# A decoder layer on one core: 64-column products in a row in the first and last units of cross-attention, and a softmax's exponential and two experts' weight casts in another place on ScalarE

## The chip, the cores and the metric

The kernel runs on one core of a Trainium2 chip. Its time is the device time of one execution in microseconds (us). A core has a matrix engine (TensorE, PE in the profile), a vector engine (VectorE, DVE), an engine for activations and copies (ScalarE, ACT), a general one (GpSimd, POOL) and one that issues most of the transfers here (SyncE, SP). Each engine takes its instructions strictly in order. An instruction that waits holds up all that is behind it on its engine. So in a kernel of this kind, where all engines work at once on different stages, the order of the instructions on each engine is a large part of the design. The change that is studied here is one of order alone.

## The reference

One decoder layer on x with 1024 tokens of width 256, in float32 (cut to what matters here):

```python
x = x + self_attention(layernorm(x))      # 16 heads of 128, weights as mxfp4 codes and scales
# cross-attention, latent form; context c: 64 rows per sequence, 64 wide
q_hk  = layernorm(x) @ Wq.T               # 16 heads of 128
q_big = einsum('bshk,hkq->bshq', q_hk, w_kc_q)        # 192 wide a head
q_big = q_big * cos_q + rotate_half(q_big) * sin_q    # rotary embedding
q_r   = q_big @ W_qr ;  kv = (c rotated)  @ W_kr      # 64 wide
p     = softmax(q_r . kv)
x     = x + (p @ c ...) @ Wo.T
# mixture of experts: 16 experts, in 4 groups; top 2 groups, then top 4 experts
xt     = layernorm(x)
scores = softmax(xt @ Wg.T)
g      = max of scores in each group;  experts outside the best 2 groups are masked
topi   = top_k(masked, 4);  w = scores at topi
y      = sum over chosen e of w_e * (silu(xt @ W1[e].T) * (xt @ W3[e].T)) @ W2[e].T
z      = (silu(xt @ Ws1.T) * (xt @ Ws3.T)) @ Ws2.T    # shared expert, inner width 352
out    = x + y + z
```

The inner width of an expert is 176.

## The kernel before, in words

Float32 products are made from pairs: each operand is split into a high part[...] and a low part, the difference. Three products (high by high, high by low, low by high) stand for one. `parts_of` (L111 to L113) makes the split: ScalarE copies the high part, and VectorE subtracts it for the low part. Every product of this kind has line L104 in the profile, and what it computes is told by the names of its tiles.

The stages follow each other: self-attention to about 200 us, cross-attention to about 408, the shared expert and the routing to about 437, then the experts. A scheduler orders each engine's instructions by a planner's estimate of when they are due, and the code corrects it by hand: under `tc.issue_after(m)`, or the shorthand `after(*ms)`, the instructions of a block are ordered behind instruction m. Such an order adds no wait on the chip between engines; it fixes who stands ahead of whom.

*Cross-attention* is cut into eight units: four heads (a "quad") by half of the tokens. The unit loop (L1155 to L1290) has ten turns, n = 0 to 9, and is pipelined: turn n computes the rotated queries of unit n, the scores of unit n - 1 and the context and output projection of unit n - 2. The parts are:

- `rotated_queries` (L990): products with w_q on PE, rotation products rt on VectorE (L1006), their sum `roped` on GpSimd (L1014);
- `pair_queries` (L1025): products with the 64-column matrix w_s (L1032), copied as q_r by ScalarE (L1045);
- `pair_scores` (L1050): scores with 64-column products (L1057), then `softmax` (L325 to L343): maximum sm_m on VectorE, eight exponentials on ScalarE (L331), sums, and the normalised pn on VectorE or GpSimd;
- `transposed` (L352 to L361): transposes of pn on PE, copies by ScalarE;
- `pair_context` (L1065): 64-column products (L1070) to c_t;
- `cross_project` (L1087): products with w_o, added to x on VectorE (L1095).

`layernorm_t` normalises the tokens and transposes them on PE (L216), with the high copy at L222 and the low at L224. In turn n = 0 the second half of the tokens is normalised and transposed for cross-attention. In turns 0 to 6 the 64-column products are ordered by hand in a row. Turns 7, 8 and 9 have a branch of their own with less order. In the late turns routing and the shared expert are woven in: `choose` (L778) picks the experts for a half of the tokens on VectorE: logits lg, group maxima, the top entries, the mask sel (L762); then PE counts earlier choices (L819 from sel, L820 from before), and VectorE works out the target rows `to` (L856). `send` (L860) scatters the tokens to the experts' rows xd in memory by transfers of GpSimd (L864), sixteen of them for the second half. `weights_of_choices` (L891) makes the routing softmax of a half: its maximum r_m (L897), the difference r_p (L899), the exponential on ScalarE (L900), and the chosen weights. silu (L937, L1342) and exp are of different table sets on ScalarE, so a change of function brings an ACT_TABLE_LOAD.

*The experts* (loop from L1407): for each, `expert_weights` loads 640 KB (w, L277), ScalarE casts the high part (L278, 1280 columns), VectorE (experts 0 to 2) or GpSimd subtracts the low (L283). `expert_inputs` (L1308) loads an expert's rows xr from xd (L1314), which waits for the scatters, and transposes them on PE (L1324) into xs; `expert_hidden` (L1333) makes the up products, silu (g, L1342 and L1345) and the product h (L1343, L1346), split as hp; `send_outputs` (L1350) makes the output y and scatters it by GpSimd. Loads of w and xr are issued by SyncE in one order.

Of the kernel before, what the change touches and what calls it, by code (L numbers as in the profile page):

```python
# [30 lines left out]
ALU = mybir.AluOpType  # L31
# [40 lines left out]
def decoder_layer(ctx: ExitStack, tc: tile.TileContext, a: dict, out: bass.AP):  # L72
# [36 lines left out]
        return [(left[0], right[0]), (left[0], right[1]), (left[1], right[0])]  # L109

    def parts_of(src, hi, lo, eng=None):  # L111
        nc.scalar.copy(hi, src)
        return (eng or nc.vector).tensor_tensor(lo, src, hi, ALU.subtract).ins  # L113


    x_pairs = [acts.tile([128, 2, D], F32, tag=f"x{n}", name=f"x{n}") for n in range(NI // 2)]
# [39 lines left out]
    variances, rstds, shifts, highs, lows = [], [], [], [], []  # L156
    norms, scaled, turned, silus, exps, softened = [], [], [], [], [], []

    def layernorm_t(which, halves=(0, 1), rows=None, meanwhile=None):


        xn_t = []
# [1 line left out]
        for half in halves:  # L164
# [47 lines left out]
            for c in range(2):  # L212
                ps = mm_tile() if which == 1 else av_tile()
                for k in range(4):
                    turned.append(
                        nc.tensor.transpose(  # L216
                            ps[:, k * 128 : (k + 1) * 128],
                            xn[k][:, c * 128 : (c + 1) * 128],
                            ident,
                        ).ins  # L220
                    )
                highs.append(nc.scalar.copy(parts[0][:, c, :], ps).ins)  # L222
                lows.append(
                    nc.vector.tensor_tensor(  # L224
                        parts[1][:, c, :], ps, parts[0][:, c, :], ALU.subtract
                    ).ins
                )
            xn_t.append(parts)
# [86 lines left out]
    with ExitStack() as attn:  # L315
# [572 lines left out]
            nc.vector.tensor_tensor(w, w, p, ALU.mult)  # L888
            return w

        def weights_of_choices(half):  # L891


            shape = [128, 4, E]
            lg = logits[half]
            m = fs.tile([128, 4], F32, tag="r_m", name="r_m")
            nc.vector.tensor_reduce(m, lg, AX.X, ALU.max)  # L897
            p = fs.tile(shape, F32, tag=f"r_p{half}", name=f"r_p{half}")
            nc.vector.tensor_tensor(p, lg, m.unsqueeze(2).broadcast_to(shape), ALU.subtract)  # L899
            exps.append(nc.scalar.activation(p, p, AF.Exp).ins)  # L900
            s = fs.tile([128, 4], F32, tag="r_s", name="r_s")
# [79 lines left out]
        with (  # L981
# [179 lines left out]
            for n in range(len(units) + 2):  # L1161
# [4 lines left out]
                roped[n] = []  # L1166
                qd, half = units[min(n, len(units) - 1)]
                rotate = iter(rotated_queries(weights[qd][0], half, roped[n]) if n in here else ())
                with after(*([projected] if n < len(units) - 1 and projected else [])):
                    pts_n = [transposed(pn) for pn in pns.pop(n - 2, ())]  # L1170
                if n < len(units) - 1:
                    roped_done = list(roped_last)
                    order = [m for m in [next(rotate, None)] if m]
                    if n - 1 in here:
# [10 lines left out]
                        c_ts.append(c_t)  # L1185
                    if n == 0:
                        with tc.issue_after(highs[-1]), tc.issue_after(lows[-1]):
                            xn_t += layernorm_t(2, (1,))
                    else:
                        pns[n - 1] = []  # L1190
                        for q_r in q_rs:
                            with after(*order):
                                pn, product = pair_scores(q_r, units[n - 1][1], nc.gpsimd)
                            order = [product]
                            pns[n - 1].append(pn)
                    if n in late:
                        with after(*order):
                            next(prep)
# [4 lines left out]
                else:  # L1203
                    if n - 1 in here:
                        q_rs, _ = pair_queries(weights[units[n - 1][0]][1], roped.pop(n - 1))
                    c_ts = [pair_context(pt, units[n - 2][1])[0] for pt in pts_n]
                    next(rotate, None)
                    if n - 1 in here:

                        eng = nc.gpsimd if n < len(units) else nc.vector  # L1210
                        pns[n - 1] = [pair_scores(q_rs[0], units[n - 1][1], eng)[0]]
                    next(rotate, None)
                    if n - 1 in here:
                        pns[n - 1].append(pair_scores(q_rs[1], units[n - 1][1], eng)[0])
# [32 lines left out]
                if n == 8:  # L1247
                    w_last = dense_weights()
                    with after(exps[-1]):
                        routed.append(weights_of_choices(0))  # L1250
                if n == 9:
                    rows[1] = [
                        xw.tile([128, 3, 2, 2, DC], F32, tag="w_s", name="rows1")
# [326 lines left out]
```

## Time and profile before

| what | us |
|---|---|
| median of 3 runs (lowest and highest) | 556.84 (555.78 to 557.23) |
| the profiled execution | 558.26 |
| its span in the trace | 556.1 |
| PE busy / its share | 524.9 / 94% |
| DVE busy / its share | 382.5 / 69% |
| ACT busy / its share | 304.3 / 55% |
| POOL busy / its share | 228.7 / 41% |
| mean granted PE clock | 0.986 of full speed |

A row of the timeline gives start and length in us, engine, line, operation, output tile, input tiles and shapes, and in brackets the idle time ahead of it with what ended that. Rows of PE's timeline count two records for one product of this kind, so that "x8" is four instructions of the code. A row of stretches gives a piece of the trace and for each engine how long it was busy there, then the clock that was granted to PE, the busy share of the transfer engines and the rate of transfers. "PEld" is the loading of weights into the matrix engine, which overlaps products.

### The profile page before, as it was taken

The numbers are of one execution on the slowest core, as the hardware profiler recorded it, in microseconds if no ns is written. First come the engines' busy times: TensorE is split into PE (matmuls) and PEld (weight loads), VectorE is DVE, ScalarE is ACT, GpSimd is POOL, SyncE is SP. The second block draws the span as 40 slices with busy tenths as digits, with TensorE's granted clock in tenths as the row PEclk, the third lists the DMA queues.
The fourth block names the chain that finished last, engine by engine and source line by source line (L and its number), as shares of the span: only waits on it lengthen the run. The fifth ranks groups of instructions, "written<-read, shape, count | busy, mean of one in ns | idle before, by whom it ended". The sixth has DMA issues, their size and how long they took to land.

```text
span 556.1 us, 10815 instructions
## 1 busy us (share of the span) xinstructions
PE 524.9 (94%) x4013; PEld 442.1 (80%) x4013; DVE 382.5 (69%) x863; ACT 304.3 (55%) x764; POOL 228.7 (41%) x213
## 2 busy tenths in 40 slices
PE   7999999999999989999999999999999879999982
PEld 6888898998989876668677686685886769999971
DVE  5465573754736799657475566758768688999967
ACT  3667575585665520625545364455735377777651
POOL 4260500101000016444342533543534737888873
PEclk9999999999999999999999999999999989999995
DMA  8553432834200779472010000000511577777366
GB/s 227 158 170 109 140 95 77 209 97 133 77 1 1 230 203 306 124 230 73 1 62 12 8 1 1 0 30 2 174 52 71 195 235 265 238 235 262 123 250 217
DMA packets 44263, 70.84 MB, mean 127 GB/s; under 512 B 11824, under 2 KB 25232, under 8 KB 44208
## 3 DMA queue, kind: packets, MB, share of 16 engines
q1 hardware_dynamic: 39376, 58.71, 35.3%
q0 software_dynamic: 3696, 10.36, 4.8%
q10 hardware_dynamic: 1136, 1.05, 0.6%
q8 instruction: 33, 0.54, 0.4%
q14 instruction: 22, 0.18, 0.1%
HBM read 48.61 MB, written 21.86 MB: 127 GB/s over the span
## 4 chain that ended last, share of the span: by engine, by line


## 5 line engine op out<-in xcount | busy, mean ns | idle before, releaser
L1014 POOL TENSOR_TENSOR roped<-rt,rt 128x512 f32<-128x512 f32 x48 | 61.8, 1309 | 52.6 <-DVE rt L1006 51.6
L104 PE MATMUL mm<-xn,w_q 128*128 128x512 f32 x288 | 72.6, 402 | 0.5 <-ACT xn L222 0.5
L1006 DVE TENSOR_TENSOR rt<-mm,rope_q 128x512 f32<-128x512 f32 x96 | 61.0, 680 | 10.8 <-PE mm L104 10.4
L104 PEld LDWEIGHTS mm<-xn,w_q 128*128 128x128 f32 x288 | 52.6, 188 | 14.3 <-issue 1.2
L104 PE MATMUL mm<-xs,w 128*128 128x384 f32 x270 | 53.8, 347 | 6.9 <-issue 2.3
L1363 POOL DMA_INDIRECT yd<-y,to x45 | 47.8, 1062 | 20.7 <-ACT y L1358 7.1
L325 DVE TENSOR_REDUCE sm_m<-at 128x8 f32<-128x512 f32 x32 | 21.9, 684 | 47.9 <-PE at L582 47.1
L104 PEld LDWEIGHTS mm<-xs,w 128*128 128x128 f32 x270 | 46.7, 192 | 9.0 <-issue 5.1
L331 ACT ACTIVATE p<-at,sm_m 128x64 f32<-128x64 f32 x128 | 38.2, 343 | 14.9 <-DVE sm_m L329 12.8
L523 POOL TENSOR_TENSOR wv<-code,scale 128x512 fp32r<-128x512 f32 x7 | 9.1, 1294 | 89.2 <-DMA scale<-in_scales 59.6
L1032 PE MATMUL mm<-roped,w_s 128*64 128x512 f32 x192 | 44.3, 599 | 0.2 <-DVE rt L1006 0.2
L360 ACT COPY pt<-at 64x512 f32<-64x512 f32 x32 | 18.6, 582 | 40.0 <-PE at L352 40.0
L565 ACT ACTIVATE qT<-mm,bqkv 128x512 f32<-128x512 f32 x32 | 21.8, 688 | 33.7 <-PE mm L104 33.7
L104 PE MATMUL mm<-wv,xn 128*128 128x256 f32 x256 | 36.2, 288 | 0.0
L104 PE MATMUL mm<-wo,o 128*128 128x256 f32 x256 | 34.1, 286 | 2.1 <-DVE x L624 2.1
L104 PE MATMUL av<-w,hp 128*128 128x256 f32 x225 | 35.1, 290 | 0.3 <-ACT y L1358 0.3
L104 PEld LDWEIGHTS mm<-wo,o 128*128 128x128 f32 x256 | 31.7, 191 | 3.7 <-DVE x L624 3.2
L104 PE MATMUL mm<-xn,wk 128*128 128x512 f32 x128 | 34.2, 399 | 0.0
L104 PE MATMUL mm<-xn,wq 128*128 128x512 f32 x128 | 33.2, 398 | 0.2
L343 POOL TENSOR_TENSOR pn<-p,sm_s 128x512 f32<-128x512 f32 x14 | 14.6, 1044 | 45.3 <-DVE sm_s L339 45.3
L104 PEld LDWEIGHTS mm<-wv,xn 128*128 128x128 f32 x256 | 32.5, 189 | 0.7
L601 PE MATMUL av<-pt,v 128*128 128x128 f32 x256 | 31.2, 275 | 1.0 <-DVE o L611 1.0
(219 smaller groups left out, 1184.3 us busy)
## 6 DMA issues: line engine op xcount, KB each, us to landing
w<-in_W SPq DMA_DIRECT2D x15, 640.0 KB
code<-in_codes SPq DMA_DIRECT2D x32, 256.0 KB
scale<-in_scales SPq DMA_DIRECT2D x32, 256.0 KB
xr<-xd SPq DMA_DIRECT2D x15, 408.0 KB
xd<-zeros SPq DMA_DIRECT2D x8, 720.0 KB
yd<-zeros SPq DMA_DIRECT2D x8, 512.0 KB
got<-yd SPq DMA_DIRECT2D x16, 256.0 KB
wq<-in_Wq SPq DMA_DIRECT2D x4, 512.0 KB
```

Source lines behind the costliest of these rows:

```text
L104: m = nc.tensor.matmul(ps, lhsT=l, rhs=r, start=(n == 0), stop=(n == len(pairs) - 1))
L325: nc.vector.tensor_reduce(m, sc, AX.X, ALU.max)
L331: last = nc.scalar.activation(p[:, b], sc[:, b], AF.Exp, bias=m[:, b : b + 1], accum_out=s[:, b : b + 1])
L343: .tensor_tensor(pn, p, s.unsqueeze(2).broadcast_to(shape), ALU.mult)
L360: nc.scalar.copy(pt[:S, :, 0, :], ps[:S])
L523: mults[n] = eng.tensor_tensor(w, *loaded[gr].pop(n), ALU.mult).ins
L565: nc.scalar.activation(qk[which][:, half * 512 : (half + 1) * 512], ps, AF.Identity, bias=bqkv[:, which, h : h + 1],).ins
L601: nc.tensor.matmul(av[:, k * 128 : (k + 1) * 128], lhsT=v[:, i, k0 : k0 + HD], rhs=pt[:, i].rearrange("p a q -> p (a q)"), start=True, sto ...
L1006: factors = nc.vector.tensor_tensor(mt, ps3, rope_table(t, 2 * ab + k), ALU.mult)
L1014: nc.gpsimd.tensor_tensor(r.rearrange("p (b s) -> p b s", s=S), one, two, op)
L1032: nc.tensor.matmul(ps[h // 2][(h % 2) * 64 : (h % 2) * 64 + 64], lhsT=w_s[:, t, blk, ab, :], rhs=roped[2 * t + ab], start=first[h], stop=l ...
L1363: sent = nc.gpsimd.indirect_dma_start(out=yd[: (E - 1) * SLOTS + min(TOPK, E - 1 - e) * NT], out_offset=bass.IndirectOffsetOnAxis(ap=to[:, ...
```

## The change

Four things are put in another order. The numbers of instructions on each engine are the same in both kernels.

1. Turn 7 of the unit loop now takes the ordered branch, like turns 0 to 6: its transposes come behind the projection, its queries' products in one row, then contexts and scores in a row. Only turns 8 and 9 remain in the other branch.
2. In turn 0 `layernorm_t` is called with `later=True`: it normalises, but its eight transposes with their copies are returned as a function, which turn 1 calls behind its scores.
3. `parts_of` notes its last high and low instruction. `weights_of_choices` is cut in two: `exps_of_choices` makes the maximum, the difference and the exponential, and for the second half of the tokens it is called in turn 9, ordered behind the casts of the dense expert's hidden; the rest stays in the expert loop.
4. The cast of the weights of expert 1 is ordered behind the last cast of expert 0's input, and that of expert 2 behind the last cast of expert 0's hidden, in both cases instead of behind the last silu. On SyncE the load of expert 3's weights comes to stand ahead of the load of expert 3's inputs.

On PE the order of turn 1 was 2 transposes, a piece of 4 products of L1032, 4 transposes, 4 products, 2 transposes, 4 products, then 16 scores; it is now 12 products, 16 scores, 8 transposes. On ScalarE the exponential of L900 with its table load comes directly behind the last cast of the shared hidden, and the table load back stands directly ahead of the first expert's silu. On VectorE the low part of w_last_up stands ahead of the routing's chain from lg to sel, and the maximum of unit 8's scores behind that chain.

```diff
     def parts_of(src, hi, lo, eng=None):
-        nc.scalar.copy(hi, src)
-        return (eng or nc.vector).tensor_tensor(lo, src, hi, ALU.subtract).ins
+        high_last[0] = nc.scalar.copy(hi, src).ins
+        low_last[0] = (eng or nc.vector).tensor_tensor(lo, src, hi, ALU.subtract).ins
+        return low_last[0]
...
-    def layernorm_t(which, halves=(0, 1), rows=None, meanwhile=None):
+    def layernorm_t(which, halves=(0, 1), rows=None, meanwhile=None, later=False):
...
+            if later:
+                return lambda xn=xn, parts=parts: [turn(xn, parts)]
+            xn_t.append(turn(xn, parts))
...
-        def weights_of_choices(half):
-
+        def exps_of_choices(half):
...
             exps.append(nc.scalar.activation(p, p, AF.Exp).ins)
+            return p
+
+        def weights_of_choices(half, p):
...
-                with after(*([projected] if n < len(units) - 1 and projected else [])):
+                with after(*([projected] if n < len(units) and projected else [])):
                     pts_n = [transposed(pn) for pn in pns.pop(n - 2, ())]
-                if n < len(units) - 1:
+                if n < len(units):
...
-                            xn_t += layernorm_t(2, (1,))
+                            turn_rest = layernorm_t(2, (1,), later=True)
...
+                    if n == 1:
+                        with after(*order):
+                            xn_t += turn_rest()
...
+                        order = [high_last[0]]
                         h_p = dense_gated(*dense_ups)
+
+                        with after(*order, high_last[0], low_last[0], silus[-1]):
+                            p_last = exps_of_choices(1)
...
-            low = lows[-1]
+            low, cast = lows[-1], high_last[0]
             hs[e - 1] = expert_hidden(ws[e - 1], xs[e - 1][0], SLOTS)
+            if e == 2:
+                cast = hidden_high
+            hidden_high = high_last[0]
...
-                with tc.issue_after(low), tc.issue_after(silus[-1]):
+
+                with tc.issue_after(low), tc.issue_after(cast if e < 3 else silus[-1]):
                     ws[e] = expert_weights(a["W123"][e], nc.vector if e < 3 else nc.gpsimd)
...
-                routed.append(weights_of_choices(1))
+                routed.append(weights_of_choices(1, p_last))
```

More of the change, by code (lines that the diff above doesn't have):

```diff
@@ L111, in parts_of @@
     def parts_of(src, hi, lo, eng=None):
-        nc.scalar.copy(hi, src)
-        return (eng or nc.vector).tensor_tensor(lo, src, hi, ALU.subtract).ins
+        high_last[0] = nc.scalar.copy(hi, src).ins
+        low_last[0] = (eng or nc.vector).tensor_tensor(lo, src, hi, ALU.subtract).ins
+        return low_last[0]
+    high_last, low_last = [None], [None]
     x_pairs = [acts.tile([128, 2, D], F32, tag=f"x{n}", name=f"x{n}") for n in range(NI // 2)]
@@ L211, in layernorm_t, with turn @@
                 order.enter_context(tc.issue_after(meanwhile(xn_t[0])))
[L212 to L219, printed above, removed]
+            def turn(xn, parts):
+                for c in range(2):
+                    ps = mm_tile() if which == 1 else av_tile()
+                    for k in range(4):
+                        turned.append(
+                            nc.tensor.transpose(
+                                ps[:, k * 128 : (k + 1) * 128],
+                                xn[k][:, c * 128 : (c + 1) * 128],
+                                ident,
+                            ).ins
+                        )
+                    highs.append(nc.scalar.copy(parts[0][:, c, :], ps).ins)
+                    lows.append(
+                        nc.vector.tensor_tensor(
+                            parts[1][:, c, :], ps, parts[0][:, c, :], ALU.subtract
                         ).ins
                     )
[L222 to L228, printed above, removed]
+                return parts
+            if later:
+                return lambda xn=xn, parts=parts: [turn(xn, parts)]
+            xn_t.append(turn(xn, parts))
             for last in (variances[-1], highs[-1]):
@@ L900, in weights_of_choices @@
             exps.append(nc.scalar.activation(p, p, AF.Exp).ins)
+            return p
+        def weights_of_choices(half, p):
+            shape = [128, 4, E]
             s = fs.tile([128, 4], F32, tag="r_s", name="r_s")
@@ L1206, in decoder_layer @@
                     c_ts = [pair_context(pt, units[n - 2][1])[0] for pt in pts_n]
-                    next(rotate, None)
                     if n - 1 in here:
-                        eng = nc.gpsimd if n < len(units) else nc.vector
-                        pns[n - 1] = [pair_scores(q_rs[0], units[n - 1][1], eng)[0]]
-                    next(rotate, None)
+                        pns[n - 1] = [pair_scores(q_rs[0], units[n - 1][1], nc.vector)[0]]
                     if n - 1 in here:
-                        pns[n - 1].append(pair_scores(q_rs[1], units[n - 1][1], eng)[0])
+                        pns[n - 1].append(pair_scores(q_rs[1], units[n - 1][1], nc.vector)[0])
                 if n - 2 in here:
@@ L1249, in decoder_layer @@
                     with after(exps[-1]):
-                        routed.append(weights_of_choices(0))
+                        routed.append(weights_of_choices(0, exps_of_choices(0)))
                 if n == 9:
```

## The prediction

> **What bounds the kernel now.** I read the page's first part, then busy time by stretches of the trace, and only then the timelines of single engines where TensorE was not busy.
>
> ```profile
> PE 524.9 (94%) x4013; PEld 442.1 (80%) x4013; DVE 382.5 (69%) x863; ACT 304.3 (55%) x764; POOL 228.7 (41%) x213
> ```
>
> TensorE (PE) is the bound almost everywhere: 524.9 of 556.1 us. It follows that a reordering can gain in three ways only: take away a stall of PE, make the PE instructions themselves shorter, or keep PE's clock up. The stretches show where there are stalls (columns: stretch, its length, then busy time of PE, weight load, DVE, ACT, POOL, granted PE clock, DMA share, GB/s):
>
> ```profile
> 437.00:460.00 23.00, 17.00 (x96) 14.91 (x95) 17.36 (x45) 13.90 (x24) 12.16 (x12) 0.93 0.70 230
> 455.00:457.00 2.00, 2.00 (x12) 1.73 (x11) 1.94 (x6) 0.27 (x1) 1.70 (x2) 0.59 0.95 237
> 457.00:459.00 2.00, 2.00 (x8) 2.00 (x7) 0.92 (x3) 1.32 (x2) 0.17 (x1) 0.56 0.85 334
> 460.00:480.00 20.00, 19.65 (x139) 19.43 (x138) 17.84 (x33) 15.62 (x34) 14.82 (x14) 1.00 0.75 258
> ```
>
> The first experts, 437 to 460, hold 6.0 us without PE work, and after them PE is 98% busy again (19.65 of 20). For about 4 us of that stretch, moreover, the granted clock is 0.56 to 0.59. So a microsecond saved there reaches the end, for what follows is PE's own work. The cross-attention's last units (344.41 to 408.15) are nearly full: their recorded stalls sum to about 1 us.
>
> PE's timeline in the worst place (start, length, operation, idle time before it and who ended it):
>
> ```profile
> 453.59 0.80 PE L104 MATMUL mm<-xs,w 128*128 128x384 f32 x3 [2.13 <-ACT xs L112]
> 455.92 0.90 PE L1324 MATMUL at<-ident,xr 128*128 128x128 f32 x3
> 456.47 2.86 PE L104 MATMUL mm<-xs,w 128*128 128x384 f32 x9
> ```
>
> PE waits 2.13 us for ScalarE's (ACT's) cast of expert 2's input. The nine products at 456.47 take 2.86 us where nine took 1.87 (447.18): the low clock. ACT's timeline says why the cast is late:
>
> ```profile
> 443.69 1.26 ACT L278 CAST w<-w 128x1280 fp32r<-128x1280 f32 x1
> ...
> 447.94 1.28 ACT L900 ACT_TABLE_LOAD   x1
> 449.31 0.26 ACT L900 ACTIVATE r_p<-r_p 128x64 f32<-128x64 f32 x1
> 449.59 1.28 ACT L1342 ACT_TABLE_LOAD   x1
> ...
> 451.90 1.26 ACT L278 CAST w<-w 128x1280 fp32r<-128x1280 f32 x1
> 453.07 0.47 ACT L112 CAST xs<-at 128x384 fp32r<-128x384 f32 x1
> ```
>
> Routing's exponential with its two table loads stands in ACT's queue for 2.94 us (447.94 to 450.88), and then a weight cast of 1.26 us stands before the input's cast.
>
> **The change, part by part.** No instruction is added or removed on any engine; all is order.
>
> *The exponential and the weight casts.* The table load and the exponential go to behind the last cast of the shared hidden (it ends at 434.54). ACT then idles 4.53 us before expert 0's input cast at 439.06, so 1.28 + 0.26 = 1.5 us are hidden there. If that cover were gone they would cost expert 0's cast 1.5. Their inputs, r_m and r_p on DVE (0.2 each), also go forward, into DVE's idle 1.50 at 435.4. The load back to silu's set can't hide with them: it stands in ACT's queue ahead of expert 0's silu, behind a wait for PE's product (442.55 in before). Thus silu begins at about 443.8 and is 1.28 late. But the cast of expert 1's weights (1.26), which stood between silu and the casts of expert 1's input, is now ahead of silu, in ACT's idle 2.27 before 442.55. The two cancel: expert 1's first input cast is ready at 445.2 instead of 445.4. Its weights' low halves (1.56 on DVE, from 444.98) fall into DVE's idle 2.13 before 443.07, and so the low parts of the input come about 1.1 sooner. Expert 1's up product, which PE finishes at 451.46 together with the output behind it, then ends at about 450.3. With the exponential and the weight cast of expert 2 out of the way, expert 2's input is cast at about 450.2 instead of 453.54. The 2.13 us stall is gone and PE is 3.3 ahead.
>
> What is late next? The transposes of expert 3's input (455.92). Their load waits for the last scatter of tokens on POOL, whose sixteen transfers take 1.27 each and don't move. SyncE's queue:
>
> ```profile
> 446.64 4.39 SPq L1314 DMA_DIRECT2D xr<-xd  x2
> 451.54 0.33 SPq L277 DMA_DIRECT2D w<-in_W  x1
> ```
>
> The second xr load of that row is issued at about 450.7; a load needs 3.3 to 3.7 us to the transposes in the earlier experts, so expert 3's can start at about 454.3. PE gets there at 452.1 and waits 2.2. Of the 3.3, 1.6 remain (455.92 to 454.3). The weights of expert 3 go ahead of that xr in SyncE's queue, at about 447.0 instead of 451.54: their buffer's release (expert 1's weights cast) is early now. If it were not, xr would wait behind it. Their cast, 457.68 in before after 2.40 of waiting for the transfer, comes at about 453.5 and limits nothing.
>
> The rest hangs on the clock. In before 451.46 to about 455 hold roughly 1.1 of PE work in 3.4 us, and the low clock follows; nine products lose 2.86 - 1.65 = 1.2. (1.65 is nine at 0.18 from start to start.) The Trainium skill, "TensorE: Matmul & The Clock Gate", Part 1, has half the clock after an idle window of about 3.4 us, free-running. The trace is harsher than "idle": a stall of 2.13 with scattered products sufficed. By the page's rule my new stall of 2.2 between full stretches would not lower the clock, and the gain is 1.6 + 1.2 = 2.8; by the row, a like stall may, and the gain is 1.6. In my order the emptiest window of 3.4 holds at least 1.2 of work, little more than before's 1.1, but in one dense piece, and 437 to 440, with 0.41 busy in its last 2 us, kept 1.00. I take 2.8 and keep 1.6.
>
> Another page speaks against that size: "ScalarE: Activation LUTs", What ACT_TABLE_LOAD costs, has 1.28 for a load and 1.38 of drain, 2.66 a switch. The row shows 1.28 and the exponential right behind (449.31), so no drain: the removed block is 2.94, not 5.6, and the load left before silu costs 1.28. By the page, silu would be 2.66 late, 1.4 not cancelled, and the gain 1.4 less where POOL's scatter doesn't bound. I go by the row.
>
> *First unit.* Second-half transposes of the norm (eight, 2 + 4 + 2) move from between the 64-column products to behind the scores. A full row is shorter:
>
> ```profile
> 222.41 1.94 PE L1032 MATMUL mm<-roped,w_s 128*64 128x512 f32 x8
> ...
> 314.42 5.43 PE L1032 MATMUL mm<-roped,w_s 128*64 128x512 f32 x24
> ```
>
> Three lone pieces of 24 records take 3 x 1.87 = 5.6 from start to start, the row 5.2: 0.4 saved, and transposes in one run save 0.1 to 0.2. But the row can't begin before DVE's last rotation product (PE waited for it up to 219.95), and the 0.44 of transposes filled that wait. Then the casts of the transposed norm come behind the first eight exponentials on ACT, and DVE's rotations behind its low parts: the second pair of L440 loses about 0.5. Net 0, with ends -0.3 and +0.8.
>
> *Last units.* Unit 7 gets the ordered row and unit 8's scores directly behind products. Rows of 64-column work joined, 344.41 to 408.15 would take 62.5 instead of 63.7: at best -1.2. But PE then comes to L819 at about 383.9 (385.45 in before), and that waits for sel on DVE:
>
> ```profile
> 379.95 1.69 DVE L113 TENSOR_TENSOR w_last<-w_last_up,w_last 128x768 fp32r<-128x768 f32 x1
> ...
> 384.61 0.22 DVE L762 TENSOR_TENSOR sel<-left,cand 128x64 f32<-128x64 f32 x1
> 384.76 0.68 DVE L325 TENSOR_REDUCE sm_m<-at 128x8 f32<-128x512 f32 x1
> ```
>
> The chain to sel holds the same work (w_last's 1.69 is now ahead of all of it instead of in its midst), so sel stays at 385.0 and PE stalls about 1.1. Unit 8's maximum sm_m falls behind the chain's tail (before, back, nth, ch), at about 387.0 instead of 384.76; its exponentials, 2.9 us on ACT, are then mixed with the casts of c_t, and the output projection stalls about 1.0. Part of both is won back, since PE has the shared products to take up: I get +0.5 at 408, ends -1.2 and +1.0. It moves the half-1 routing, the scatters and all behind it alike.
>
> Sum: 0 + 0.5 - 2.8 = -2.3. Against the profiled execution's own time, 558.26 (556.1 of span and 2.2 around it), that is 556.0; against the median of the runs, 556.84, which is 1.4 below the profiled one, **554.5**.
>
> **Rivals.**
> *A, the clock falls all the same* after the new stall before expert 3, or later stretches take it back: experts -1.6, last units +0.5, so -1.1: 555.7. For it: the like stall in before. Against: a dense piece on both sides.
> *B, the last units win too*, since the routing chain starts sooner (its logits come from products that are sooner in PE's order): -1.2 - 2.8 = -4.0, 552.8. Against: w_last's 1.69 ahead of the chain.
> *C, slower: unit 8's softmax.* In before, the DVE finished sm_m before sel's tail, and PE had products left for the 2.3 us that it now comes later. Two softmaxes run one after the other (unit 8's two pairs of heads, 384.76 and 391.61). If the delay of 2.3 goes through both and PE has run out of other work, it costs 2 x 2.3 = 4.6 and, with DVE's w_last ahead of sel, 1.7 more: +6.3 - 2.8 = +3.5, 560.3. It decides from a loss of 4.5 in the last units (2.8 of gain and 1.7 that can be measured). For it: DVE is 12.29 of 16.00 busy from 344 to 360 and strictly in order. Against: 24 shared products of 0.25 (ws) stand behind as fill.
> *D, nothing changes*, the scatter of POOL bounds the experts earlier than I think (every xr load waits for it, not just expert 3's) and the last units cost their 0.5 to 1.0: -0.8 + 0.8 = 0: 556.8.
>
> **How the numbers follow.** 0.3% of 556.84 is 1.7 us, about what a measurement of this kernel can tell from no change. Chances: my forecast 0.36, A 0.20, B 0.10, C 0.20, D 0.14. Faster by over 0.3% (below 555.2): the forecast's greater part (0.31), B, and 0.05 of A: 0.46. Slower (above 558.5): C's greater part and little else, 0.18. Same: 0.36. The range: B's end below, 552.6, and C as far as 559.4 above, about a tenth left out on each side. Both signs hold chance; the forecast's own range is 553.7 to 555.6.
>
> **What would show it.** Right: in the changed profile ACT's exponential and its load lie in the idle time before expert 0's input cast, one table load stands just ahead of the first expert silu, no PE stall for expert 2's xs, a stall of about 2 for expert 3's xr, and a granted clock of 1.00 from 437 to 460. The 64-column row of unit 1 is 5.4 long. Wrong: low clock at 455 still, sel later than 385.5 by a microsecond, or a new stall of w_o or L352 products between 388 and 402 of over 2 us.

## The result and the profile after

The changed kernel is slower. Over 20 runs of each, its median is 557.71 us and that of the kernel before 556.01; the ratio is 1.0028, with a 95% interval of 1.0017 to 1.0039, which is 1.0 to 2.2 us. The forecast was 554.5, faster by 2.3.

The profiled execution took 558.43 with a span of 556.3; that of the kernel before, 558.26 with 556.1. The two profiles are thus no further apart than 0.2, although the medians are 1.7 apart. The profiled execution of the kernel before was 2.2 above the median of its own 20 runs, that of the changed kernel 0.7. Single traces are therefore read here for where work waits, and times from medians.

Nearly equal spans hide two differences of opposite sign. The first expert's transposes start at 432.95 in the changed kernel and at 437.09 in the kernel before, 4.1 sooner. From there to the end of PE's last product the changed kernel takes 114.5 us (to 547.46), the kernel before 111.7 (to 548.82). So the loss is in the experts.

The first part of the page, changed kernel: PE is the bound, as before.

```profile
PE 523.3 (94%) x4013; PEld 443.2 (80%) x4013; DVE 384.4 (69%) x863; ACT 304.9 (55%) x764; POOL 228.2 (41%) x213
```

The busy time by stretches, changed kernel (columns: stretch, its length, then PE, weight load, DVE, ACT, POOL, granted clock, DMA share, GB/s):

```profile
447.00:448.00 1.00, 1.00 (x8) 0.81 (x8) 0.96 (x4) 1.00 (x5) 0.29 (x1) 1.00 0.49 196
448.00:449.00 1.00, 0.67 (x5) 0.43 (x4) 1.00 (x4) 1.00 (x3) 0.69 (x2) 1.00 0.00 0
450.00:452.00 2.00, 0.00 (x0) 0.00 (x0) 1.97 (x3) 0.00 (x0) 1.81 (x3) 0.70 0.95 291
452.00:454.00 2.00, 1.18 (x5) 1.21 (x6) 0.19 (x1) 0.21 (x1) 1.05 (x1) 0.50 0.95 324
454.00:456.00 2.00, 2.00 (x8) 2.00 (x7) 0.56 (x1) 0.27 (x1) 0.00 (x0) 0.50 0.98 352
```

PE does nothing at all from 450 to 452 while the transfer engines are 95% busy, and then works at half clock. PE's timeline of the place:

```profile
446.84 0.78 PE L104 MATMUL mm<-xs,w 128*128 128x384 f32 x3
447.49 1.18 PE L104 MATMUL av<-w,hp 128*128 128x256 f32 x7
452.82 0.87 PE L1342 MATMUL at<-ident,xr 128*128 128x128 f32 x3 [4.15 <-DMA xr<-xd]
453.35 3.23 PE L104 MATMUL mm<-xs,w 128*128 128x384 f32 x9
```

Expert 2's products (446.84) follow without a wait: the stall of 2.13 at ScalarE's cast is gone. In its place PE waits 4.15 us for expert 3's rows, and the nine products behind it take 3.23 at the low clock. ScalarE's timeline shows that its part went as planned:

```profile
430.70 1.28 ACT L908 ACT_TABLE_LOAD   x1
431.99 0.26 ACT L908 ACTIVATE r_p<-r_p 128x64 f32<-128x64 f32 x1
...
434.28 1.27 ACT L287 CAST w<-w 128x1280 fp32r<-128x1280 f32 x1
438.14 1.28 ACT L1360 ACT_TABLE_LOAD   x1 [2.59 <-PE mm L104]
439.43 0.49 ACT L1360 ACTIVATE g<-mm 128x384 f32<-128x384 f32 x1
```

The exponential and its table load lie where ScalarE idled, the weight cast stands ahead of the silu, and the load back costs the silu its 1.28. What went wrong is in SyncE's queue. Here xr is an expert's rows and w its weights; the rows of expert 2, the weights of expert 3, then the rows of experts 3 and 4:

```profile
442.15 0.32 SPq L1332 DMA_DIRECT2D xr<-xd  x1
442.60 0.36 SPq L286 DMA_DIRECT2D w<-in_W  x1
448.80 0.82 SPq L1332 DMA_DIRECT2D xr<-xd  x2
```

and POOL's last scatter of tokens, for which expert 3's rows wait:

```profile
443.45 0.96 POOL L873 DMA_INDIRECT xd<-rows,to  x1 [0.30 <-issue]
```

The 640 KB of weights are issued at 442.60, before the last scatter starts at 443.45. The rows are issued 5.35 us after that start. In the kernel before the same interval was 3.04, with the weights behind (issued at 451.54):

```profile
447.68 0.96 POOL L864 DMA_INDIRECT xd<-rows,to  x1 [0.30 <-issue]
450.72 0.32 SPq L1314 DMA_DIRECT2D xr<-xd  x1
```

What SyncE waits for in front of the rows is the landing of the scatters: its longest wait of this kind is 5.7 us in the changed kernel and 3.2 in the kernel before. By the stretches of the changed kernel, the transfer engines do not fall silent until the second half of 447, and the issue follows 1.3 later.

### The profile page after: what moved, and what is told of

The parts are those of the page before. It is cut to its first block, busy times and chain, and to the rows that moved or that the text cites. A ratio compares the mean times of both kernels' runs of the same rounds, so it can differ in the third digit from the quotient of the medians.

```text
span 556.3 us, 10813 instructions
## 1 busy us (share of the span) xinstructions
PE 523.3 (94%) x4013; PEld 443.2 (80%) x4013; DVE 384.4 (69%) x863; ACT 304.9 (55%) x764; POOL 228.2 (41%) x213
## 4 chain that ended last, share of the span: by engine, by line
PE 75%; DVE 8%; DMA 5%; issue 4%; POOL 4%; ACT 3%; SPq 1%; DVEq 0%; ACTq 0%; POOLq 0%
PE mm L104 42%; PE mm L1046 8%; PE av L610 4%; PE av L104 4%; PE at L591 3%; PE at L361 3%; PE av L1084 3%; POOL xd L873 3%; PE at L1071 2%; DVE rt L1020 2%; PE mm L471 1%; DMA scale<-in_scales 1%; DMA xd<-rows,to 1%; PE mm L449 1%; PE at L1342 1%
## 5 line engine op out<-in xcount | busy, mean ns | idle before, releaser
L104 PE MATMUL mm<-xs,w 128*128 128x384 f32 x270 | 55.2, 350 | 4.4 <-ACT w L287 2.1
L1046 PEld LDWEIGHTS mm<-roped,w_s 128*64 128x64 f32 x192 | 14.8, 136 | 24.1 <-issue 23.5
```

What stands on the lines that cost most here:

```text
L104: m = nc.tensor.matmul(ps, lhsT=l, rhs=r, start=(n == 0), stop=(n == len(pairs) - 1))
L1046: nc.tensor.matmul(ps[h // 2][(h % 2) * 64 : (h % 2) * 64 + 64], lhsT=w_s[:, t, blk, ab, :], rhs=roped[2 * t + ab], start=first[h], stop=l ...
```

## Experiments

I started from this theory (1): the early release of a weight buffer lets the load of expert 3's weights go ahead of the last scatters; these land later, and the gain is lost there. The rival (2): the cross-attention's new order is what costs. Each kernel below is one of the two with the shown edit. Ratios are to the kernel before, run beside it on the same chip, with their 95% intervals. The runs came in five rounds, each on a chip of its own; a comparison within a round is safer than one across rounds.

**Parts of the change alone.** The edits are the parts themselves: the cross-attention's hunks alone; both of the experts' hunks; the exponential's; the weight casts'.

> Only the cross-attention's part: first and last units in the new order, exponential and weight casts where they were. Theory 1 (the transfer of expert 3's weights, now ahead of expert 3's rows, slows the last scatters, and the experts lose what the rest gains): 1 to 2.5 us faster than before (ratio 0.996 to 0.998), shared products at 408 sooner by 2. Theory 2 (the cross-attention's new order is what costs): 1.5 us slower, ratio 1.003.

> Only the experts' part: exponential and both weight casts sooner, cross-attention as before. Theory 1: 2 to 4 us slower, ratio 1.004 to 1.007, with a PE stall of 4 us at the transposes of expert 3's rows and a low clock after it. Theory 2: no slower than before, ratio 0.995 to 1.000.

> Only the exponential of the second half of the tokens sooner; the loads keep their order. Theory 1: 0 to 1.5 us faster, ratio 0.997 to 1.000, since 2.94 us leave ScalarE's queue ahead of expert 1 but the rows of expert 3 are no sooner. Theory 2: the same as theory 1.

> Only the casts of the weights of experts 1 and 2 sooner, with the load of expert 3's weights ahead of that of expert 3's rows; the exponential stays in the expert loop. Theory 1: slower by 2 to 4 us, ratio 1.004 to 1.007, like both together, since it holds the change of the loads' order. Theory 2: within 1 us of before.

| kernel | median, us | before, us | ratio |
|---|---|---|---|
| cross-attention alone | 555.30 | 556.22 | 0.9981 (0.9965 to 0.9997) |
| experts' part | 559.41 | 556.22 | 1.0069 (1.0050 to 1.0088) |
| exponential alone | 556.75 | 556.22 | 1.0002 (0.9988 to 1.0015) |
| weight casts alone | 559.65 | 556.22 | 1.0070 (1.0042 to 1.0097) |

The rival falls: the cross-attention gains. The exponential gives nothing measurable, and the weight casts cost all that the experts' part does. In both kernels with early casts PE waits for expert 3's rows, 3.29 and 2.37 us. With the exponential alone PE doesn't wait for these rows at all. There ScalarE's delay has only been shared out between two experts:

```profile
443.38 1.33 PE L104 MATMUL mm<-xs,w 128*128 128x384 f32 x3 [1.91 <-ACT xs L112]
...
452.53 0.80 PE L104 MATMUL mm<-xs,w 128*128 128x384 f32 x3 [1.09 <-ACT xs L112]
```

The stall ahead of expert 2's products fell from 2.13 to 1.09, and the one ahead of expert 1's grew from 1.11 to 1.91, behind a silu that now has the table load in front of it.

**The order of two loads alone.** In the kernel before, the load of expert 3's weights is issued ahead of expert 3's rows; all other instructions on all engines keep their order. (`weight_parts` hands its casts to `hold_casts`, which issues them later, and notes its load in `w_load`.)

```diff
+            if e == 3:
+                held = []
+                hold_casts[0] = held.append
+                ws[e] = expert_weights(a["W123"][e], nc.gpsimd)
+                hold_casts[0] = None
+                with tc.issue_after(low), tc.issue_after(w_load[0]):
+                    xs[e] = expert_inputs(e)
+                with tc.issue_after(low), tc.issue_after(silus[-1]):
+                    held[0]()
```

In the other two, the load goes back behind the rows, once with the casts alone and once in the changed kernel:

```diff
+                last_load = [tc.issue_after(xr_load[0])] if e == 3 else []
-                with tc.issue_after(low), tc.issue_after(cast if e < 3 else silus[-1]):
+                with ExitStack() as held, tc.issue_after(low), tc.issue_after(
+                    cast if e < 3 else silus[-1]
+                ):
+                    for h in last_load:
+                        held.enter_context(h)
```

And the changed kernel without the early casts, so with the old order of loads:

```diff
-                with tc.issue_after(low), tc.issue_after(cast if e < 3 else silus[-1]):
+                with tc.issue_after(low), tc.issue_after(silus[-1]):
```

> The kernel before with two instructions swapped and nothing else: on SyncE the load of expert 3's weights ahead of the load of expert 3's rows. Theory L (the loads' order is what costs: 640 KB run beside the last scatters, which land later, and the rows wait for these): 2 to 4 us slower than before, ratio 1.004 to 1.007, rows of expert 3 issued 3.5 us or more behind the last scatter instead of 2.1 to 2.6. Rival C (the casts' new places, and the order of PE's products that the scheduler made of them, cost): within 0.5 us of before.

> Both weight casts sooner as in the run with the casts alone, but expert 3's weights loaded behind expert 3's rows, as in before; no other instruction differs from that run. Theory L: 0 to 1.5 us faster than before, ratio 0.997 to 1.000. Rival C: 3 to 4 us slower, 1.005 to 1.007, as with the loads swapped.

> The changed kernel with one swap undone: expert 3's weights are loaded behind expert 3's rows. Theory L: 1 to 3 us faster than before, ratio 0.995 to 0.998, and faster than the changed kernel by 2.5 to 4. Rival C: as the changed kernel, 1.003.

> The changed kernel without the weight casts' new places (so with the loads' old order too): cross-attention and exponential as changed. Both theories: 0.996 to 0.999, the cross-attention's 1.1 us and little for the exponential. If this is faster than the run with the one swap undone, the early casts cost something of their own.

| kernel | median, us | before, us | ratio |
|---|---|---|---|
| before, the two loads swapped | 557.29 | 556.05 | 1.0025 (1.0009 to 1.0040) |
| casts alone, loads in the old order | 558.25 | 556.05 | 1.0037 (1.0023 to 1.0051) |
| changed, loads in the old order | 555.03 | 556.05 | 0.9989 (0.9966 to 1.0012) |
| changed, without early casts | 555.06 | 556.05 | 0.9976 (0.9955 to 0.9997) |

The swap by itself costs 0.25%, 1.4 us, less than the 2 to 4 that I expected. Undone in the changed kernel it brings back 1.0028 - 0.9989 = 0.39%, 2.2 us, the whole of the loss; whether more than that can't be told, since 0.9989 has 1 in its interval. These two ratios are from different rounds. My theory as I had put it is too simple: with the casts alone, the old order of loads leaves a loss of 0.37%, where I had expected at most none. So the swap is enough to turn the changed kernel slow, and early casts have a second cost when nothing else is moved. The kernel with the loads swapped, SyncE (the first xr is expert 2's) and POOL's last scatter:

```profile
443.83 0.32 SPq L1321 DMA_DIRECT2D xr<-xd  x1
444.28 0.34 SPq L279 DMA_DIRECT2D w<-in_W  x1
449.99 0.79 SPq L1321 DMA_DIRECT2D xr<-xd  x2
```

```profile
444.73 0.96 POOL L871 DMA_INDIRECT xd<-rows,to  x1 [0.30 <-issue]
```

The interval is 449.99 - 444.73 = 5.26, as in the changed kernel.

**What the second cost is: a later load?** With early casts and the old order of loads, expert 4's weights and expert 5's rows are loaded early too (449.45 and 449.94; in the cross-attention's kernel 451.58 and 453.50), beside expert 3's weights. With the casts alone and the old order, ScalarE's cast of expert 3's weights waited long, and the cast of expert 3's input stood behind it:

```profile
449.46 0.94 ACT L112 CAST hp<-h 128x384 fp32r<-128x384 f32 x2
455.23 1.26 ACT L287 CAST w<-w 128x1280 fp32r<-128x1280 f32 x1 [4.83 <-DMA w<-in_W]
456.39 0.85 ACT L112 CAST xs<-at 128x384 fp32r<-128x384 f32 x2
```

So I held those two loads until expert 3's weights had been cast, with one wait more and no other change of order:

```diff
-        nc.sync.dma_start(out=t, in_=src)
-        nc.scalar.copy(w[0], t)
+        load = w_load[0] = nc.sync.dma_start(out=t, in_=src).ins
+        if hold[0]:
+            behind(load, hold)
+        w_high[0] = nc.scalar.copy(w[0], t).ins
...
+                    hold[0] = w_high[0] if e == 4 else None
```

> The run with early casts and the old order of loads, with one wait more: the load of expert 4's weights (and the rows of expert 5 behind it on SyncE) is held until expert 3's weights have been cast. Theory T (what early casts cost is that buffers come free early, so that the loads of expert 4's weights and expert 5's rows run beside that of expert 3's weights, which lands 6.7 us after its issue instead of 5.3): back to 0.997 to 1.000 of before, expert 3's weights in under 5.5 us. Rival C (the order of PE's products and the casts' places): as without the wait, 1.003 to 1.005, or slower by the wait.

> The changed kernel with expert 3's weights loaded behind its rows, and with the same one wait for the load of expert 4's weights. Theory T: 0.995 to 0.998 of before, the best so far. Rival C: 0.999 as without the wait, or slower.

The ratios are 1.0051 (1.0031 to 1.0071) with the casts alone and 0.9997 (0.9983 to 1.0011) in the changed kernel with the old order of loads. Neither is better than without the wait, and expert 3's weights still took 7.2 us (issued 449.01, cast 456.21). That theory falls.

**The two ends of cross-attention.** The hunks of the first units alone, and of the last units alone.

> Only the first units' part: transposes of the second half of the norm behind unit 0's scores. By the prediction's step 0 us (-0.3 to +0.8), ratio 0.999 to 1.0015; if the first part of the profile of the changed kernel is typical, 0.8 us faster, 0.9985.

> Only the last units' part: turn 7 of the unit loop in the ordered branch. By the prediction's step +0.5 us (-1.2 to +1.0), ratio 0.998 to 1.002; if the stall at the counts of the earlier choices is as short as in the changed kernel's profile, 1.2 us faster, 0.998.

First units: 0.9992 (0.9975 to 1.0009), not told from no change. Last units: 0.9971 (0.9956 to 0.9986), which is 1.6 us faster by the ratio (medians 554.16 and 556.14). It is the lowest ratio of the study, though its interval overlaps those of the next ones, and the last rounds below show that this gain does not hold everywhere.

**Each early cast alone, and half a load.** In the first two, `cast if e < 3` becomes `cast if e == 1`, with the new and with the old order of loads; in the third it is `cast if e == 2`. In the last, the kernel before loads 640 of the 1280 columns of expert 3's weights ahead of the rows and the rest behind.

> The changed kernel with only expert 1's cast early; expert 2's is back. The load of expert 3's weights is ahead of its rows here, and the order of experts 4 to 9 is that without early casts. Theory S (swapped loads 1.4 to 2.2 us, order of experts 4 to 9 0.7 to 0.9, nothing else): 1.000 to 1.0015 of before, last scatter to the issue of expert 3's rows 4.7 us or more. Rival W (expert 1's early cast costs something by itself): 1.002 or more.

> The same with expert 3's weights loaded behind its rows. Theory S: 0.995 to 0.998 of before, faster by 1.4 to 2.2 us than the run above. Rival W: 0.999 or more.

> The changed kernel with only expert 2's cast early; loads in the old order, experts 4 to 9 in the changed kernel's kind of order. Theory S: 0.998 to 1.0005 of before, 0.7 to 0.9 us slower than the changed kernel without early casts (0.9976), and the stretch from the 72nd to the 144th record of the up products 23.3 us or more, where kernels without the early cast have 22.7. Rival W: as without early casts, 0.9976, and 22.7.

> The kernel before with half of expert 3's weights loaded ahead of its rows and the other half behind. If the swap costs by the bytes beside the last scatters: from the last scatter to the issue of expert 3's rows about 4.2 us, between the 3.0 to 3.6 of the old order and the 5.3 of the whole load ahead. If it is the place in the queue alone that matters: 5.3, or 3.0 to 3.6.

The half load, SyncE and POOL:

```profile
446.58 0.12 SPq L281 DMA_DIRECT2D w<-in_W  x1
451.43 0.32 SPq L1328 DMA_DIRECT2D xr<-xd  x1
451.80 0.43 SPq L284 DMA_DIRECT2D w<-in_W  x1
```

```profile
447.25 0.96 POOL L878 DMA_INDIRECT xd<-rows,to  x1 [0.30 <-issue]
```

The interval is 451.43 - 447.25 = 4.18, half way between 3.04 and 5.26. That speaks for the bytes and against the place in the queue, but it is one trace. Over the traces it was 2.9 to 4.0 in thirteen with the old order and 4.75 to 5.67 in the five with the whole load ahead. So 4.18 lies only just above what the old order gives. One trace has the old order and 4.91 (the changed kernel without early casts); there the rows of expert 2, 408 KB, were themselves issued 0.7 behind the last scatter's start.

The three ratios: expert 1's cast, new order of loads, 1.0051 (1.0030 to 1.0073); the same, old order, 1.0021 (1.0002 to 1.0039); expert 2's cast, 1.0047 (1.0026 to 1.0069). The difference of the first two is again the swap, 0.30%, within one round, though their intervals overlap. But all three are 0.4% or so above what I expected, so neither theory had its numbers. Their traces all hold a PE wait of 2.6 to 3.3 us in the last units of cross-attention, for ScalarE's copies, which the earlier traces of the same order did not have, and which lies ahead of all that these kernels differ by. With expert 2's cast early the stretch of the expectation was 23.45, in the two others 22.6: theory S had that right. To see whether the idle time stays, I ran two of the kernels side by side again.

> The changed kernel without early casts, once more. If the idle time of ScalarE in the last units goes with the chip that runs it: 0.996 to 0.999 of before where the trace shows none, 1.000 to 1.003 where it shows one of 2 to 3 us.

> With expert 1's early cast and the old order of loads, once more, beside the run above. Theory S: within 0.8 us of the run above or faster (0.3 to 1 us faster by the traces, 118.6 against 119.1 from the first expert's rows to the end). Rival W: slower than the run above by 1 us or more.

Without early casts: 1.0072 (1.0050 to 1.0093), where the same kernel had 0.9976 on another chip, and where I had expected 1.003 at most. So a ratio of this kernel moved by 1% from one round to another. With expert 1's cast and the old order of loads: 1.0029 (1.0010 to 1.0047), close to the 1.0021 of the round ahead. Within this round expert 1's early cast gains 0.43%, 2.4 us, so the rival that it costs by itself falls there. I had expected at most 1. The wait is there again. ScalarE in the last units, first in the earlier trace of the kernel without early casts, then in the second:

```profile
395.03 0.62 ACT L112 CAST w_last<-w_last_down 128x512 fp32r<-128x512 f32 x1 [1.43 <-DMA w_last_down<-in_W]
396.26 0.59 ACT L112 CAST c_t<-av 128x512 fp32r<-128x512 f32 x1 [0.62 <-PE av L1084]
```

```profile
394.43 0.62 ACT L112 CAST w_last<-w_last_down 128x512 fp32r<-128x512 f32 x1 [1.38 <-DMA w_last_down<-in_W]
398.29 0.58 ACT L112 CAST c_t<-av 128x512 fp32r<-128x512 f32 x1 [3.24 <-PE mm L104]
400.46 0.58 ACT L369 COPY pt<-at 64x512 f32<-64x512 f32 x1 [1.59 <-PE mm L104]
```

PE had made c_t's input by 395.7 in the second (products at 394.57, 1.09 long). ScalarE still began its copy at 398.29, and idled 1.59 once more before the next one. What the row names as the end of its wait, a product on PE, was not needed by either. PE had no product left:

```profile
401.70 1.09 PE L1084 MATMUL av<-pt,kv 128*64 128x128 f32 x16 [2.65 <-ACT pt L370]
```

## Why the prediction was wrong, point by point

**The step that failed** is the cost of expert 3's weights: they go ahead of the rows in SyncE's queue, at about 447.0, and that "limits nothing", while the scatters on POOL "don't move". The place of the load was right: 447.0 is 0.7 ahead of the last scatter's start in the kernel before (447.68), and 442.60 is 0.85 ahead of it in the changed one (443.45). What I looked at was only whether the load's own landing was early enough. It ran beside the scatters that expert 3's rows wait for, and I put that at nothing without a reason. I had asked what an early buffer sets off, and not what that collides with. The scatter's interval grew from 3.04 to 5.35, and PE's new stall was 4.15 instead of 2.2. The swap is worth 1.4 us alone and 2.2 in the changed kernel, about what turns the sign: with the swap undone the kernel stands at 0.9989, with the swap at 1.0028. The measured 557.71 lies in the range of my forecast, but on the side that I had given to rival C, for another reason.

**ScalarE's queue** was read rightly, its worth was not. The 2.13 stall went, table load and weight cast cancelled before the first silu, and the load took 1.28 without a drain, as the row had it. But the exponential alone moved the time by nothing (1.0002). Without the early weight casts the table load was not cancelled, and half of the stall moved to expert 1. With them, in the changed kernel, the rows of expert 3 set the pace, so that 2.94 us left a queue that was no longer the last to be waited for.

**The clock.** I took the low clock of before, 1.2 us, as gone. It fell again, from 451 to 458, as rival A had it. Of the twenty profiles thirteen have half clock somewhere from 440 to 462, for 3.4, 6.8 or 10.2 us, and seven have none, the kernel with both experts' parts among the seven, despite a stall of 3.29. One kernel, that with expert 1's cast and the old order of loads, has none in its first trace and some in its second. So what one profile shows is a draw, and the term should have been in the range and not in the sum. But the order sets the odds. The mean granted clock over all runs was 0.9841 to 0.9847 for the kernel before in the first three rounds, 0.9831 with the swap alone, 0.9830 for the changed kernel, and 0.9856 for the changed kernel with the loads back. A stretch at half clock lowers the mean by half of its share. So, as an estimate, the last two differ by 2 x 0.0026 x 555 = 2.9 us at half clock, in which PE does 1.4 us less work. Up to 1.4 of the 2.2 us that the swap costs there, and by the same sum up to 0.9 of the 1.4 that it costs alone, may thus come by way of the clock. The rule of a free-running window of about 3.4 us (the Trainium skill, "TensorE: Matmul & The Clock Gate", Part 1) agrees with lengths that are 3.4 and its multiples, and with the scatter of the places, better than my reading of one idle stretch.

**The base.** The same holds for the whole trace: I subtracted the stalls of one execution, 558.26, from a median of 556.84, and 20 runs put the median at 556.01. Where that execution was late can be seen. The kernel with the two loads swapped has the same order on every engine up to the experts, and its first expert's transposes start at 434.68 instead of 437.09. In the profile of the kernel before ScalarE and VectorE each idled once on the way with their inputs made (c_t's at 401.54, left at 421.83):

```profile
404.33 0.59 ACT L112 CAST c_t<-av 128x512 fp32r<-128x512 f32 x1 [1.39 <-PE mm L104]
423.13 0.22 DVE L762 TENSOR_TENSOR sel<-left,cand 128x64 f32<-128x64 f32 x1 [1.30 <-DVE left L761]
```

With the loads swapped the same two instructions start without idle time, at 402.87 and 420.36. So 2.4 of the 4.1 us by which the changed trace leads at the first expert are no gain of the change.

**The last units**: rival B, that they win too, was right here, in sign. The stretch from 344 to the shared products, before and changed:

```profile
344.41:408.15 63.74, 62.79 (x454) 47.41 (x453) 46.86 (x149) 35.64 (x132) 26.35 (x23) 1.00 0.15 49
```

```profile
343.57:406.14 62.57, 62.47 (x454) 47.80 (x453) 47.82 (x149) 35.57 (x132) 26.25 (x23) 1.00 0.16 50
```

62.57 is my best case, 62.5, to a tenth, but the gain is half of what these rows say. In the other traces of the old order the stretch takes 63.2 (seven traces; the half load's has 63.7), in those of the new order 62.6 (six traces without the idle time of the last rounds, 65.9 to 68.0 in the five with it). So 0.6 is the new order and 0.6 ScalarE's idle time in the profile of the kernel before. The stall at the count of the earlier choices that I put at 1.1 isn't there:

```profile
384.45 0.43 PE L828 MATMUL av<-sel,upto 128*128 128x64 f32 x2
...
388.31 3.13 PE L104 MATMUL mm<-w_o,c_t 128*128 128x256 f32 x24
```

sel ended at 383.4 where I had 385.0. Nor does the projection stall. Unit 8's maximum did fall behind the chain's tail, but the chain came sooner and left it where it was: 384.85 for the first pair of heads, where the kernel before has 384.76 and I had 387.0, and 387.99 for the second, 3.6 sooner than the 391.61 of before:

```profile
384.85 0.68 DVE L334 TENSOR_REDUCE sm_m<-at 128x8 f32<-128x512 f32 x1
387.99 0.69 DVE L334 TENSOR_REDUCE sm_m<-at 128x8 f32<-128x512 f32 x1
```

The term had the wrong sign: -0.6 by the traces, and -1.6 by the ratio of the last units alone, for +0.5. It was no part of the loss.

**The first unit**: a row of 5.37, and a wait of 0.68 ahead of it, as forecast. The trace gives 0.8 up to 343.57, but over all traces that point comes at 343.6 to 344.4 with the old order and at 343.2 to 344.6 with the new one; the time, 0.9992, can't tell that from the forecast 0.

**Rival C**, slower by the last units' softmax, named the right side for a wrong reason: the delay of 2.3 that it feared isn't there (384.85), and where the last units were run alone they gained. The losses in the last two rounds come with ScalarE's idle time, which is no part of that rival. **Rival D** had the scatters as what binds the experts, which they do here, but it saw no more than a gain lost.

**What stays open.** Early casts alone, with the old order of loads, cost 2.1 us. When the exponential is moved too, they cost at most little (0.9989 against 0.9976, intervals that overlap). The traces show that with expert 2's cast early the scheduler orders experts 4 to 9 otherwise: from the 72nd to the 144th record of the up products, counted from nought, 23.3 to 24.1 us in eight kernels, against 22.6 to 23.0 in ten of the twelve traces without it and 23.4 in the other two, for the same 156 records of PE. In that stretch PE waits 0.6 to 0.8 in sum in seven of the eight and 1.1 in the eighth, in most of them for a weight cast; the two traces with 23.4 hold a wait of 0.6 too. This is in the traces; as a time of its own it wasn't resolved, for in the last runs the kernel with expert 2's cast was not slower than the one without early casts. The rest of the 2.1 is not explained. How much of the 20 runs of the changed kernel had ScalarE's idle time isn't known either; its profile has none.

## What to carry to other kernels

When an instruction is moved forward, follow the buffer that it frees to the transfer that waits for it, and ask which transfers that one will run beside: a load that nobody needs yet, beside a scatter that somebody waits for, can cost more than the move gains. Hold such a load behind the urgent one in the issuing queue; that is one order and no wait. And take stalls that one profiled execution shows, and low clock above all, as a sample: two or three profiles of the kernel before tell which of them are there to be gained, and the mean clock over many runs tells what an order does to it.

## What the runs showed that I had not expected

The landing of the scatters is held back by a plain load that runs beside them: against the 3.04 of the kernel before by 1.1 us with 320 KB (one trace), and by 1.7 to 2.6 with 640 KB (five traces). The old order itself spreads over 2.9 to 4.0, so the growth with the bytes is likely and not shown. That transfer engines take turns between queues packet by packet, as the Trainium skill, "DMA: Bandwidth & Descriptors", Queues, rings and completion order, has it, would give a delay that grows with the bytes; no run here shows the turns themselves.

ScalarE can idle for 3.2 to 4.7 us, 2.6 to 4.0 of them with its input ready. It did so at one place in all of the five last profiles that have the last units' new order, and in none of the earlier ones. In these last rounds the kernel before itself took 558.6 and 559.4 instead of 556. The profile of the kernel before is of this kind too. Seven traces (this one, the half load's and the last five) have idle time of 1.3 to 1.8 on VectorE ahead of the mask sel (at 422 to 426), and the other thirteen have none. So it is not a matter of the new order alone. In the traces of that order, with the idle time and without, one packet of 16 KB of instructions arrives between 393 and 396, within about a microsecond of the issue of two weight loads of 640 KB. A late instruction fetch would look like this, but no run here separates it, nor the chip from the hour.
